# Six places where TensorE waits in a graph-attention and attention kernel: a store reordered behind a read, and work moved or turned at the two ends

## The chip, the cores and the metric

The kernel runs on one core of a Trainium2 chip. The metric is the device time in microseconds of one execution; three executions of the kernel before took 3074.83, 3075.51 and 3082.33 us. A core has five engines that work side by side, each in the order of its own instruction list: TensorE (PE) for matrix products, VectorE (DVE), ScalarE (ACT), GpSimd (POOL), and SyncE (SP), which here only issues DMAs. They wait for one another through semaphores.

## The reference

x holds 32 batches of 512 nodes with 512 features; adj is one 512 x 512 mask for all. Two layers follow each other, each with a residual and a layer norm without weights:

```python
# layer 0: one graph attention head of width 256
h = x @ W                                            # 512 -> 256
e = leaky_relu((h @ a[0]) + (h @ a[1]).T, 0.2)       # 512 x 512
out = softmax(e + NEG * (1 - adj)) @ h
x = layernorm(x + concat([out, h]))
# layer 1: eight heads of width 64
q, k, v = split(x @ Wq.T + bq), split(x @ Wk.T + bk), split(x @ Wv.T + bv)
attn = softmax(where(adj == 0, -inf, q @ k.T / 8))
x = layernorm(x + merge(attn @ v) @ Wo.T + bo)
```

All is float32. The 32 batches don't depend on each other.

## The kernel before, in words

A batch b is worked in four passes of a pair of heads, hp = 0 to 3; (b,hp) names one pass. A pass makes the scores of both heads for four blocks of 128 queries (`head_scores`, L684): a matmul (L699), the row minimum of the masked negative scores on VectorE (L315), the exponential with its sum on ScalarE (L708). The weights so made must be turned, keys to partitions, before they can multiply the values. There are two ways:

- `head_blocks` (L720): VectorE transposes blocks of 32 x 32 (L330), eight instructions a pair, and SP issues 16 DMAs of 128 KB (L347) that move the blocks from tile t to their places in tile pt. There is one buffer of t and one of pt.
- `head_turn` (L729): TensorE transposes the eight tiles as matmuls with the identity (32 of them, L736) into PSUM, and VectorE and ScalarE copy four tiles each into pt (L737). The set `turned` (L981) lists the pairs done so.

The product of one pair with the values, `head_values` (L751, the matmuls of tile pav at L757), stands in the pass after it, behind that pass's scores. It is multiplied on VectorE (L769) by the inverse sums, which go through memory: written by SP as d_tot (L717), read back by GpSimd's queue (L748).

Between these stand the other parts, cut in steps and laid out by hand: the projections of queries and keys (`project_two`, tile pw, L545, four products per half batch with copies L569 by ScalarE and an add L598 by GpSimd) and of values (`project_v`, pv); layer 0 of the batch after (`l0_...`, tiles ph, et, po); and the end of the batch before: seven products of the output weights (`finish_seven`, pf, L789), the statistics (L280), `out_norm` (L890; two small steps on VectorE, then four activations L900) and `store` (L908). Every engine runs its instructions in the order in which the program lists them, and SP its DMAs likewise, so a DMA that has to wait holds back those behind it. A DMA also waits until the eighth one before it on SP's queue has landed. Buffers come from pools that turn round: x has three, so `load_x(b + 2)` writes where batch b - 1 lay, and waits for its store.

Layer 0 of batch b + 2 is begun in the pass hp = 3 of batch b: `l0_columns` writes the two attention columns to memory and reads them back as rows on all partitions (L389, L391); `l0_maxima` finds each row's bound; `l0_write` (L421, 2 KB) and `l0_read` (L426, 256 KB) bring it back as a row, from which `l0_row` (L434, GpSimd) makes a term of the scores in the next batch's first pass. `l0_weights` (L466) subtracts it and takes exponentials, `l0_values` (L472) makes the product po. `l0_add_h` (L375) adds h to the residual, four GpSimd instructions.

The opening (L922 to L964) does batch 0's layer 0, batch 1's projection in four products (`second`), and `x1_first` (L501), which turns the normed x of batch 0 with TensorE, four tiles px, each copied by ScalarE (L510). The end (L1095 to L1106) makes the last batch's output product directly: `last_products` (L853) adds the residual and three of four blocks of features, `last_product` the fourth, which needs the last pair, and `last_norm` norms each block and stores it.

Of the kernel before, what the change touches and what calls it, by code (L numbers as in the profile page):

```python
# [26 lines left out]
def kernel(  # L27
# [117 lines left out]
    def load_x(b):  # L145
        x_sb = io.tile([P, NB, F], F32, name=f"x_{b}", tag="x", bufs=3)
        nc.sync.dma_start(x_sb, x[b].rearrange("(c p) f -> p c f", p=P))
        st["x1", b] = x_sb
# [17 lines left out]
    for g in range(4):  # L166
        nc.sync.dma_start(
            adjp_sb[g * G : (g + 1) * G],
            adj[g * P : (g + 1) * P].rearrange("(i q) n -> q i n", q=G),
        )  # L170
    nc.sync.dma_start(wo_sb, wot.rearrange("(c p) d -> p c d", p=P))
    load_x(1)
    nc.gpsimd.dma_start(bq_sb, bq)
    nc.gpsimd.dma_start(bk_sb, bk)
    with nc.allow_non_contiguous_dma(reason="512 numbers, once"):
# [182 lines left out]
    def l0_product(b, i):  # L358
        xt_sb = st["xt", b]
        ph = ps_m.tile([P, 2 + F1], F32, name=f"ph_{b}_{i}", tag="m")  # L360
        matmul_f(ph, lambda c: xt_sb[:, c, i * P : (i + 1) * P], lambda c: w_sb[:, c, :])
        return ph
# [12 lines left out]
    def l0_add_h(b):  # L375

        h_sb, z = st["h", b], st["x1", b]
        for i in range(NB):
            nc.gpsimd.tensor_tensor(
                z[:, i, F1:], z[:, i, F1:], h_sb[:, i, 2 : F1 + 2], ALU.add  # L380
            )
# [42 lines left out]
    def l0_read(b):  # L424

        nc.sync.dma_start(  # L426
            st["rows", b][:, 1], st["least", b].partition_broadcast(P)
        )
# [69 lines left out]
        move_one(x1t.rearrange("p g c (i q) -> p g c i q", i=NB), t)  # L498
        st["x1t", b] = x1t

    def x1_first():  # L501

        z = st["x1", 0]
        x1t = act.tile([P, 4, FC, NB * G], F32, name="x1t_0", tag="x1t")
        for i in range(NB):
            px = psum_s(f"px_{i}")
            for c in range(FC):
                cols = slice(c * P, (c + 1) * P)
                nc.tensor.transpose(px[:, cols], z[:, i, cols], ident)
            nc.scalar.copy(  # L510
                x1t[:, :, :, i * G : (i + 1) * G].rearrange("p g c q -> p c g q"),
                px.rearrange("p (c g q) -> p c g q", c=FC, g=4),
            )
        st["x1t", 0] = x1t
# [236 lines left out]
    def head_values(b, hp, bank=None):  # L751
        pt, inv = st.pop(("pt", b, hp)), st.pop(("inv", b, hp))
        po = (bank or psum)(f"pav_{b}_{hp}")
        for c in range(NB):
            for j in range(2):
                head = 2 * hp + j
                nc.tensor.matmul(  # L757
                    po[j * D : (j + 1) * D, :],
                    st["v", b, c // 2][:, c % 2, head * D : (head + 1) * D],
                    pt[:, :, j, c, :, :].rearrange("p g i q -> p g (i q)"),  # L760
                    start=(c == 0),
                    stop=(c == NB - 1),
                )
        if hp % 2 == 0:
            st["ot", b, hp // 2] = act.tile(
                [P, 2, N], F32, name=f"ot_{b}_{hp // 2}", tag="ot", bufs=3
            )
        ot = st["ot", b, hp // 2][:, hp % 2]
        nc.vector.tensor_tensor(  # L769
            ot.rearrange("p (g i q) -> p g i q", g=4, i=NB),  # L770
            po.rearrange("p (g i q) -> p g i q", g=4, i=NB),
            inv.rearrange("p (g q) i -> p g i q", g=4),
            ALU.mult,
        )
# [133 lines left out]
    def store(b):  # L908
        nc.sync.dma_start(out[b].rearrange("(c p) f -> p c f", p=P), st["x1", b])
# [7 lines left out]
    def steps(todo):  # L917
        for _ in todo:
            pass
# [18 lines left out]
    for i in range(NB):  # L938
        l0_values(0, i)
        ln_stats(st["x1", 0], "0_0", i)  # L940
        if i == NB - 1:
            second.append(l0_product(1, 3))
            for k in range(NB):
                l0_copy(1, k, second[k])
        ln_root("0_0", [i])
        if i == 1:
            weight_negative(QUERIES)
        if i > 0:
            l0_norm(0, [i - 1])
    l0_norm(0, [NB - 1])  # L950
    x1_first()
    l0_columns(1)
    x1_sums(0, nc.vector)
    weight_sums(VALUES, nc.vector)
# [23 lines left out]
        nc.vector.tensor_tensor(bo_sb, pb, bo_sb, ALU.add)  # L978

    before = None  # L980
    turned = {(B - 2, 2), (B - 1, 2), (B - 1, 3)}  # L981
    for b in range(B):
        more = b < B - 1
        seven = finish_seven(b - 1) if b > 0 else None
        for hp in range(NP):

            head_scores(b, hp, 0)
            head_scores(b, hp, 1)  # L990
            if hp == 0:
                values = project_v(b)
                next(values)
                if more:
                    l0_scores(b + 1, [0, 1])
                if b == 0:
                    l0_add_h(1)
            elif hp == 1:
                if b == 0:
                    l0_output(1)  # L1000
                else:
                    if more:
                        l0_weights(b + 1)
                    next(seven)
            elif hp == 2:
                if b > 0:
                    next(seven)
                if b > 0 and more:
                    add_bias(b + 1)
            else:  # L1010
                if b > 0:
                    if b + 2 >= B:
                        steps(seven)
                    if not more:
                        output_weights()
                    out_stats(b - 1)
                else:
                    weight_sums(OUTPUT, nc.gpsimd)
                    add_bias(0)
                if b + 2 < B:  # L1020
                    for i in range(NB):
                        l0_project(b + 2, i)
                    l0_columns(b + 2)
                if b > 0:
                    ln_root(f"1_{b - 1}")
            head_scores(b, hp, 2)
            head_scores(b, hp, 3)
            if b > 0 and hp in (1, 2):
                next(seven)
            if b > 0 and hp == 3:  # L1030
                out_norm(b - 1)
            if (b, hp) not in turned:
                head_blocks(b, hp)
            if before is not None:
                head_values(*before)
            if (b, hp) in turned:
                head_turn(b, hp)
            if hp == 0:
                if more:
                    l0_row(b + 1)  # L1040
                    leaky(st["row", b + 1])
                next(values)
                head_inverse(b, 0)
                if b > 0 and more:
                    l0_add_h(b + 1)
                if more:
                    l0_scores(b + 1, [2, 3])
                steps(values)
                if b == 0:
                    l0_weights(1)  # L1050
            elif hp == 1:
                head_inverse(b, 1)
                if b > 0 and more:
                    next(seven)
                    l0_output(b + 1)
                if b + 2 < B:
                    load_xt(b + 2)
                two = project_two(b, 1)
                next(two)
                if more:  # L1060
                    l0_norm(b + 1)
                next(two)
                blocks = x1_blocks(b + 1) if more else None
                for part in (blocks, two, blocks, two, blocks):
                    if part:
                        next(part, None)
                if not more:
                    next(seven)
            elif hp == 2:
                if b == 0:  # L1070
                    output_bias()
                else:
                    next(seven)
                    if b + 2 < B:
                        steps(seven)
                head_inverse(b, 2)
                if more:
                    x1_sums(b + 1, nc.gpsimd)
            else:
                if b + 2 < B:  # L1080
                    l0_maxima(b + 2)
                    l0_write(b + 2)
                if b > 0:
                    store(b - 1)
                if b + 2 < B:
                    l0_read(b + 2)
                    load_x(b + 2)
                if more:
                    steps(project_two(b + 1, 0))
                head_inverse(b, 3)  # L1090
                if b == 0:
                    weight_negative(OUTPUT)
                    add_bias(1)
            before = (b, hp)
    b = B - 1  # L1095
    for i in range(NB):
        last_products(b, i)
    head_values(b, 3, psum_s)
    norms = []
# [66 lines left out]
```

## Time and profile before

| | |
|---|---|
| median of three executions | 3075.51 us |
| the profiled execution's own time | 3080.21 us |
| its span, first to last instruction | 3078.4 us |
| TensorE busy | 3039.4 us |
| VectorE, ScalarE, GpSimd busy | 2490.8, 1537.7, 1251.6 us |
| mean granted clock of TensorE | 0.996 |
| DMA issues of pt moves | 2000, 128 KB each, landing after 3.4 us (median) |

A profile is one execution. Busy time is the time in which an engine executed; what it waited for stands in the list of waits, as `engine tile line <- releaser: us in total, times, longest us`. A line of the timeline reads: start, duration, engine, line of the kernel, operation, `out<-in` tiles, shape, the count of merged instructions, and in brackets the idle time before the first and what ended it. A duration of merged instructions runs from the first start to the last end, or to the window's edge. DMAs stand as issues of the queue SPq. The granted clock says which share of TensorE's full rate it was given in a stretch.

### The profile page before, as it was taken

Reading aid. Unit: us, or ns where it says so; the run is one execution under the profiler, and the core shown is the slowest. Engines: PE = TensorE matmul, PEld = TensorE weight load, DVE = VectorE, ACT = ScalarE, POOL = GpSimd, SP = SyncE. Lnnn points to the kernel's source line nnn. Section 1 sums busy time; section 2 is a strip of 40 time slices with the busy share of each in tenths; the row PEclk is TensorE's granted clock in tenths of the full one; section 3 lists DMA queues with packets and bytes.
Section 4 is the critical chain, followed back from the end, with each engine's and each line's share of the span. In section 5 each row is a group of like instructions: output and inputs, shape, how many; then the busy total and the mean of one; then the engine's idle time right before and its main releaser. Section 6 shows DMA issues by size and latency. Waiting matters only on the chain. (4 is left out here: it accounts for less than half of the span.)

```text
span 3078.4 us, 44731 instructions
## 1 busy us (share of the span) xinstructions
PE 3039.4 (99%) x13460; PEld 2065.7 (67%) x13460; DVE 2490.8 (81%) x5711; ACT 1537.7 (50%) x3262; POOL 1251.6 (41%) x1224
## 2 busy tenths in 40 slices
PE   8999999999999999999999999999999999999998
PEld 6566666666666666666666666666666666666654
DVE  6788888888878887888888888878888888888865
ACT  4355554545544545544455545455444555454544
POOL 4343444443343434444433434344444334343422
PEclk9999999999999999999999999999999999999999
DMA  6556666566575666665666755666656667556632
GB/s 180 142 138 157 156 164 154 138 164 159 145 177 135 152 156 160 159 158 136 168 155 147 176 142 148 156 156 158 160 138 168 151 150 177 143 143 155 157 93 66
DMA packets 245633, 464.64 MB, mean 151 GB/s; under 512 B 94800, under 2 KB 97360, under 8 KB 245392
## 3 DMA queue, kind: packets, MB, share of 16 engines
q1 hardware_dynamic: 232928, 427.93, 56.1%
q0 software_dynamic: 12464, 33.84, 4.1%
q8 instruction: 109, 1.79, 0.3%
q14 instruction: 132, 1.08, 0.1%
HBM read 132.65 MB, written 34.27 MB: 54 GB/s over the span
## 5 line engine op out<-in xcount | busy, mean ns | idle before, releaser
L708 ACT ACTIVATE p<-p,least 128x512 f32<-128x512 f32 x1024 | 725.8, 711 | 509.8 <-DVE least L315 192.7
L315 DVE CUSTOM_DVE_ANT_0 p<-ps,mask 128x512 f32<-128x512 f32 x1024 | 644.9, 685 | 219.0 <-PE ps L699 218.7
L330 DVE STREAM_TRANSPOSE t<-p 128x512 f32<-128x512 f32 x1000 | 607.7, 674 | 10.2 <-issue 5.5
L699 PE MATMUL ps<-qk 64*128 64x512 f32 x2048 | 511.3, 615 | 0.3 <-DVE least L315 0.3
L757 PE MATMUL pav<-pt,v 128*64 128x512 f32 x2048 | 469.8, 600 | 12.7 <-DMA d_att<-att 6.2
L748 POOL DMA_DIRECT2D inv<-d_tot x256 | 134.4, 530 | 587.3 <-DMA d_tot<-tot 273.7
L757 PEld LDWEIGHTS pav<-pt,v 128*64 128x64 f32 x2048 | 139.2, 137 | 328.8 <-issue 289.6
L699 PEld LDWEIGHTS ps<-qk 64*128 64x128 f32 x2048 | 179.3, 186 | 206.3 <-issue 152.2
L459 POOL TENSOR_TENSOR et<-et,mask0t 128x512 f32<-128x512 f32 x126 | 143.9, 1155 | 324.7 <-ACT et L455 324.7
L812 POOL TENSOR_TENSOR x<-x,u_o 128x512 f32<-128x512 f32 x93 | 117.0, 1273 | 303.2 <-ACT u_o L807 271.8
L477 PE MATMUL po<-h,et 128*128 128x257 f32 x1024 | 234.0, 387 | 3.5 <-ACT et L470 2.9
L264 PE MATMUL ph<-w_sb,xt 128*128 128x258 f32 x1024 | 235.0, 387 | 0.3 <-DVE w_sb L190 0.3
L477 PEld LDWEIGHTS po<-h,et 128*128 128x128 f32 x1024 | 190.3, 191 | 59.8 <-issue 28.0
L264 PEld LDWEIGHTS ph<-w_sb,xt 128*128 128x128 f32 x1024 | 193.3, 191 | 51.4 <-PE ps L699 22.0
L534 POOL TENSOR_TENSOR x<-x,bo_sb 128x512 f32<-128x512 f32 x128 | 158.5, 1271 | 92.0 <-DVE x1t_b L330 92.0
L708 ACT ACTIVATION_READ_ACCUMULATOR p<-p,least 128x1 f32 x1024 | 192.5, 188 | 0.0
L708 ACT ACT_TABLE_LOAD x63 | 80.8, 1283 | 220.0 <-DVE least L315 219.5
L286 ACT ACTIVATE rstd<-mv,eps 128x4 f32<-128x4 f32 (+1 forms) x66 | 19.6, 297 | 335.8 <-DVE mv L281 332.8
L789 PE MATMUL pf<-wo_sb,ot 128*128 128x256 f32 x744 | 182.2, 388 | 0.0
L789 PE MATMUL pf<-wox_sb,ot 128*128 128x256 f32 x744 | 179.0, 383 | 0.0
L789 PEld LDWEIGHTS pf<-wo_sb,ot 128*128 128x128 f32 x744 | 136.2, 190 | 63.0 <-DVE least L315 23.5
L280 DVE BATCH_NORM_STATS2 stats<-x 128x6 f32<-128x512 f32 x252 | 171.8, 682 | 7.8 <-POOL x L812 3.0
(155 smaller groups left out, 5386.1 us busy)
## 6 DMA issues: line engine op xcount, KB each, us to landing
pt<-t SPq DMA_DIRECT2D x2000, 128.0 KB, 3.4
x<-in_x_dram SPq DMA_DIRECT2D x32, 1024.0 KB, 5.6
inv<-d_tot POOLq DMA_DIRECT2D x256, 128.0 KB, 3.8
xt<-in_xt_dram SPq DMA_DIRECT2D x31, 1024.0 KB, 5.4
x1t<-x1t_b SPq DMA_DIRECT2D x496, 64.0 KB, 2.0
out_dram<-x SPq DMA_DIRECT2D x31, 1024.0 KB, 5.7
rows<-d_att SPq DMA_DIRECT2D x31, 512.0 KB, 3.8
rows<-d_least SPq DMA_DIRECT2D x31, 256.0 KB, 4.2
```

Source lines behind the costliest of these rows:

```text
L264: nc.tensor.matmul(ps, lhs(c), rhs(c), start=(c == 0), stop=(c == FC - 1))
L280: nc.vector.bn_stats(stats, z[:, i, :])
L315: nc.vector.tensor_tensor_reduce(out=out, in0=scores, in1=mask, scale=-1.0, scalar=MIN_INIT, op0=ALU.add, op1=ALU.min, accum_out=least,)
L330: nc.vector.transpose(t[:, :, :, i, :].rearrange("p r c q -> p c r q"), src.rearrange("p (c r k) -> p c r k", r=4, k=G),)
L459: engine.tensor_tensor(et[:, j, :], et[:, j, :], mask0t[:, j, :], ALU.add)
L477: nc.tensor.matmul(po, et[:, j, i * P : (i + 1) * P], h_sb[:, j, 2:], start=(j == 0), stop=(j == NB - 1),)
L534: nc.gpsimd.tensor_tensor(z[:, i, :], z[:, i, :], bo_sb, ALU.add)
L699: nc.tensor.matmul(ps, qk[rows, 0, i * P : (i + 1) * P], qk[rows, 1, :], start=True, stop=True)
L708: nc.scalar.activation(p, p, AF.Exp, bias=least, scale=-1.0, accum_out=total[:, j, i : i + 1])
L748: nc.gpsimd.dma_start(inv[j * D : (j + 1) * D], d[j].partition_broadcast(D))
L757: nc.tensor.matmul(po[j * D : (j + 1) * D, :], st["v", b, c // 2][:, c % 2, head * D : (head + 1) * D], pt[:, :, j, c, :, :].rearrange("p ...
L789: nc.tensor.matmul(ps[:, k * half : (k + 1) * half], columns[:, c, k * P : (k + 1) * P], weights(c), start=start and k == 0 and c == 0, st ...
```

## The change

Six edits:

- **Opening, loads.** x of batch 1 is loaded ahead of the output weights wo_sb.
- **Opening, layer 0.** The fourth product of batch 1's projection moves from ahead of all four px tiles to between the second tile's transposes and its copy. Its copy to h and `l0_add_h(1)` follow `x1_first`; the latter stood in pass (0,0), behind the first scores of batch 1's layer 0.
- **Pair (0,2)** is turned by TensorE: `head_turn` in place of `head_blocks`, and so behind `head_values(0,1)` rather than ahead of it.
- **Each batch's end, on SP:** `l0_write`, `l0_read`, `store`, `load_x`, where `store` stood ahead of `l0_read`. This concerns batches 1 to 29.
- **Batch 30:** `out_norm(29)` moves from behind the scores of pass (30,3) into `project_two(31, 0)`, behind its first step with its four copies on ScalarE; `store(29)` follows it.
- **Batch 31:** `out_norm(30)` and `store(30)` move behind the loop. The first two `last_products` move ahead of the turning of pair (31,3).

```diff
+    load_x(1)
     nc.sync.dma_start(wo_sb, wot.rearrange("(c p) d -> p c d", p=P))
-    load_x(1)
...
-    def x1_first():
+    def x1_first(between):
...
                 nc.tensor.transpose(px[:, cols], z[:, i, cols], ident)
+            if i == 1:
+                between()
             nc.scalar.copy(
...
         if i == NB - 1:
-            second.append(l0_product(1, 3))
-            for k in range(NB):
+            for k in range(NB - 1):
                 l0_copy(1, k, second[k])
...
-    x1_first()
+    x1_first(lambda: second.append(l0_product(1, 3)))
+    l0_copy(1, 3, second[3])
+    l0_add_h(1)
     l0_columns(1)
...
-    turned = {(B - 2, 2), (B - 1, 2), (B - 1, 3)}
+    turned = {(0, 2), (B - 2, 2), (B - 1, 2), (B - 1, 3)}
...
-                if b == 0:
-                    l0_add_h(1)
...
-            if b > 0 and hp == 3:
+            if b > 0 and hp == 3 and b + 2 < B:
                 out_norm(b - 1)
             if (b, hp) not in turned:
                 head_blocks(b, hp)
             if before is not None:
                 head_values(*before)
+            if (b, hp) == (B - 1, 3):
+                last_products(b, 0)
+                last_products(b, 1)
             if (b, hp) in turned:
                 head_turn(b, hp)
...
                 if b + 2 < B:
                     l0_maxima(b + 2)
                     l0_write(b + 2)
-                if b > 0:
+                    l0_read(b + 2)
+                if b > 0 and b + 2 < B:
                     store(b - 1)
                 if b + 2 < B:
-                    l0_read(b + 2)
                     load_x(b + 2)
                 if more:
-                    steps(project_two(b + 1, 0))
+                    two = project_two(b + 1, 0)
+                    next(two)
+                    if b + 2 >= B:
+                        out_norm(b - 1)
+                        store(b - 1)
+                    steps(two)
...
     b = B - 1
-    for i in range(NB):
+    out_norm(b - 1)
+    store(b - 1)
+    for i in (2, 3):
         last_products(b, i)
```

## The prediction

> **What bounds the kernel now.** First the page: busy shares, then the 40 slices.
>
> ```profile
> PE 3039.4 (99%) x13460; PEld 2065.7 (67%) x13460; DVE 2490.8 (81%) x5711; ACT 1537.7 (50%) x3262; POOL 1251.6 (41%) x1224
> PE   8999999999999999999999999999999999999998
> ```
>
> TensorE sets the time; only the first and last slices show it idle. So the second view is the list of its own waits, longest in total first (total us, times, longest).
>
> ```profile
> PE pav L757 <- DMA d_att<-att: 6.2, 2, 5.0
> PE pw L545 <- ACT p L569: 4.8, 1, 4.8
> PE pav L757 <- DMA d_least<-least: 3.6, 4, 1.5
> PE po L477 <- ACT et L470: 2.9, 1, 2.9
> PE px L509 <- DVE rstd L291: 1.6, 1, 1.6
> PE pt L736 <- DVE pt L737: 1.5, 2, 1.2
> ```
>
> These are nearly all the 39 us that TensorE is not busy (3078.4 - 3039.4), and each can be looked up in the timeline. The edits sit at these six places. The pav that waited "for d_att" waits for the pair (0,2), whose last move lands 0.3 us before it.
>
> ```profile
> 67.58 2.60 POOL L379 TENSOR_TENSOR x<-x,h 128x256 f32<-128x256 f32 x4
> 70.14 2.11 POOL L434 TENSOR_TENSOR row<-rows 128x512 f32<-128x512 f32 x1
> 77.44 2.38 ACT L470 ACTIVATE et<-et 128x512 f32<-128x512 f32 x4 [4.54 <-DVE et L469]
> 78.21 9.21 PE L477 MATMUL po<-h,et 128*128 128x257 f32 x32 [2.86 <-ACT et L470]
> ...
> 133.55 5.77 PE L757 MATMUL pav<-pt,v 128*64 128x512 f32 x16 [4.99 <-DMA d_att<-att]
> ...
> 2959.35 2.91 ACT L900 ACTIVATE x<-x,shift,rstd 128x512 f32<-128x512 f32 x4
> 2962.17 1.53 ACT L569 COPY p<-pw 128x512 f32<-128x512 f32 x3
> 2962.88 2.05 PE L545 MATMUL pw<-tx,wqx_sb 128*128 128x256 f32 x4 [4.75 <-ACT p L569]
> ...
> 3024.83 3.90 PE L736 MATMUL pt<-ident,p 128*128 128x128 f32 x32
> ```
>
> A second cost hides behind the long waits: the work after them is slow (pav 5.77 us instead of 3.65, four pw matmuls 2.05 instead of 1.03). The granted clock by 5 us window was 0.73 and 0.93 from 40 us, 0.68 from 80, 0.60 and 0.72 from 130, 0.57 and 0.75 from 2960, and 1.00 nearly everywhere between.
>
> The last place recurs. SP's queue at the end of one batch:
>
> ```profile
> 2030.51 0.53 SPq L421 DMA_DIRECT2D d_least<-least  x1
> 2031.15 0.38 SPq L909 DMA_DIRECT2D out_dram<-x  x1
> 2035.13 0.33 SPq L426 DMA_DIRECT2D rows<-d_least  x1
> 2037.20 0.37 SPq L147 DMA_DIRECT2D x<-in_x_dram  x1
> 2040.10 0.36 SPq L717 DMA_DIRECT2D d_tot<-tot  x1
> ```
>
> The store goes out 1.3 us after the last move of pair (b,3); the move landed 4.4 us after the write's issue, the pav at 2034.94 waited 1.47.
>
> **The skill.** The Trainium skill, "TensorE: Matmul & The Clock Gate", Part 1 (The HAM clock gate), says the array falls to half rate after a mostly idle window of about 3.4 us, and stays there until a busy one. The trace agrees: each low stretch above sums to about 3.4 or 6.8 us at half rate ((1-0.60)x5 + (1-0.72)x5 = 3.4 us of clock lost). "DMA: Bandwidth & Descriptors", Queues, rings and completion order, says that a DMA's semaphore lands only after every earlier write of the same DMA engine. The trace agrees: the 2 KB write landed in 1.40 us in the opening, but in 3.3 to 4.6 us in most batches, behind moves and beside the store. "SBUF — State Buffer", Who interferes with whom, says a GpSimd operation and a VectorE one in a two-port mode exclude each other; here the norm L296 took 1.07 us at 36.82 beside GpSimd work and 0.55 elsewhere.
>
> **The change, part by part** (us on TensorE's own order).
>
> *Opening, px.* The fourth product of batch 1 (8 matmuls, 1.91) moves into the 1.56 hole behind px1. px2 still waits for VectorE's norms (40.14), and pw for the last copy (42.18), so nothing is gained directly. But TensorE is then busy some 2.5 of the 3.4 us before 42.3 instead of 1.3, so the half-rate window (42.3 to 45.7, 1.7 lost) should go. Against it: the four adds of h (2.60) now run on GpSimd from 39.1, beside the norms at 39.59 and 40.24, which I charge 0.8 (twice the 0.5 seen at 36.82, part of it in slack). x of batch 1 is issued ahead of wo_sb to be there; wo_sb is not read until about 114. The fourth copy and att come about 0.5 later on ScalarE, hidden by GpSimd's busy p add before L404. Net -0.9 (0 to -1.7).
>
> *h added early.* The row L434 starts at 67.6 instead of 70.14. Then VectorE's leaky starts at 70.05 instead of 72.29; value results to 74.15; subtractions 74.15 to 76.9, the last two paced by GpSimd's masks, which end at 76.0 (its inverse issue still waits for d_tot, 72.6). Exponentials end at 77.6 instead of 79.8: -2.2. The half-rate window from 79.8 (1.7) should go too. But VectorE then is the limit: statistics end 85.6 instead of 89.0, 3.4 earlier, and pair (0,1), with 0.54 of slack at its pav, follows VectorE. -3.5 (-2 to -4).
>
> *Pair (0,2) turned.* Added on TensorE: 32 transposes, 3.90 as at 3024.83. Removed: the wait 4.99 and half rate in the pav, 5.77 - 3.65 = 2.12. VectorE gives 8 block transposes (4.86) for 4 copies (about 2.7), ScalarE takes 4 copies (2.4) in a gap of 6.2, SP loses 16 moves (10 us). 3.90 - 7.11 = -3.2. The pav then comes at 132.4, and pw at 136.0 finds tx ready (GpSimd, 129.8). Next late would be pair (0,3): slack 5.06, of which 3.2 and 0.6 (its blocks start later) are used. Range -2 to -4.
>
> *Read, then store, then load.* 29 times. Removed: the store from beside the last moves of (b,3). From their last issue those land in 3.49 on average, the other pairs' in 2.93 to 3.14. The (b,3) waits sum to 4.5 over nine batches; I expect 3.2 of it to go. Added: SP now waits for the write's landing (about 2.5) before the store, so the load, which waits for the store (about 5.7), goes out some 2.3 later, at 8.6 after the write instead of 6.3. Behind it on SP stand d_tot and the 16 moves of (b+1,0), released by VectorE at 8.9 to 10.8: just free. The load lands 3.7 after the first move instead of 1.4; the seventh move needs its landing and goes at 3.7. Over 30 batches the landing of the last move hardly follows the load's (correlation 0.34), so I take 0.4 later; the slack of (b,0) is 1.7 on average, 0.45 at least: 0.2 lost in all. -3.0 (+23 to -4.5; see the rivals).
>
> *Norms behind the copies, batch 30.* The four L900 (2.91) go behind p1, p5, p7, u2. p1 ends at 2959.95, TensorE resumes at 2960.05 instead of 2962.88, and part or all of the slow 2.3 goes. But pair (30,3) lands at 2975.6, 0.35 earlier now that VectorE skips two small steps, against a pav at 2977.99: no more than 2.4 + 0.35. -2.7 (-1.5 to -4).
>
> *End.* From the end of pav (31,2), 3043.26, to pav (31,3), 3063.69, are 20.4. The work in it is 3.9 of transposes and 4 x 3.44 = 13.8 of products. Two products (6.9) now cover the exponentials (done at 3046.7) and the copies; their third block needs ot (31,2) at 3045.8, ready at 3045.4. -2.8. The inverses should land near 3061.5, 3 before they are used; the norms and store of batch 30 run under the last products.
>
> Sum: -0.9 - 3.5 - 3.2 - 3.0 - 2.7 - 2.8 = -16.1, in the profiled execution 3078.4 to 3062.3 of span. Its own time was 3080.2, 4.7 above the median 3075.5 of the three runs, which all I expect to shift alike: 3059.4.
>
> **Rivals.** *The load comes too late (slower).* At the head of each (b,0) the load and the moves share the DMA engines. If the last move follows the load fully, 2.3 late, the 29 slacks in the trace leave 18.3 of waits, and I land at 3075.5 - 13.1 + 18.3 = 3080.7; at 2.5 late 23.7 and 3086. It decides from 2.0 late on (11.2 of waits, no gain left to measure). For it: the seventh move waits for the load. Against: moves go one per 0.63 us, so a backlog drains, and load landings from -0.1 to +2.8 left the last move at 12.3 to 13.9. *The opening's gains are absorbed.* VectorE is over 90% busy from 90 to 120; if half rate stays in the opening and (0,2) finds GpSimd or SP behind it, 7.6 there become 2, and the end 3065. *The tail and batch 30 are held by landings:* pair (30,3) or the inverses come late, 4 lost: 3063.4. *Reorder without effect* (other traffic makes the tails late): 3062.4.
>
> **How the numbers follow.** Forecast, everything roughly as summed, 0.66; no effect of the reorder or landings in the tail 0.14; opening absorbed 0.10; load too late 0.10, half of it slower. About 0.3%, 9.2 us, is what a measurement can tell from no change, so faster means under 3066.3. It follows from the first two cases and 0.05 of the third: 0.85; slower 0.05; the same 0.10. The range: part ranges added in quadrature give about 4; downward all half-rate windows gone, 3053; upward the absorbed opening and a load 1.5 late (3.3 of waits), 3069.
>
> **What would show it.** Right: no wait above 1 us at po near 76, at pav (0,2), at pt of the last pair; no half-rate stretch near 80 and 131; 1984 moves instead of 2000 and 992 block transposes instead of 1000; L900 of batch 30 behind L569; the read issued 2.5 after the write. Wrong: new waits of pav (b,0) behind x<-in_x_dram, or a pair (0,3), (30,3) that takes over the wait.

## The result and the profile after

The changed kernel is slower: 3086.90 us median of 8 executions (3082.68 to 3089.06) against 3076.39 (3074.08 to 3082.33) for the kernel before on the same chip, a ratio of 1.0030 [1.0019, 1.0041]. Forecast were 3059.4 us and a range of 3053 to 3069. The profiled execution took 3083.0 us (3080.21 before), one of the shortest of the eight; its span is 3081.2 us (3078.4).

The page first, its busy shares and the row of TensorE in 40 slices.

```profile
PE 3038.7 (99%) x13492; PEld 2070.5 (67%) x13492; DVE 2530.2 (82%) x5707; ACT 1549.4 (50%) x3266; POOL 1249.4 (41%) x1224
PE   8999999999999999999999999999999999999999
```

TensorE does 0.7 us less and the last slice is now full, so the end did improve. The span is 2.8 longer all the same. TensorE's waits, in the form in which they were shown of before (total us, times, longest):

```profile
PE pav L759 <- ACT et L470: 10.0, 12, 2.6
...
PE pav L759 <- DMA pt<-t: 3.5, 7, 0.9
PE pav L759 <- issue: 3.2, 4, 2.0
PE po L477 <- ACT et L470: 2.2, 1, 2.2
...
PE pw L547 <- ACT p L571: 1.9, 1, 1.9
PE px L509 <- DVE inv L485: 1.5, 1, 1.5
```

Of the two long ones, the one that was put down to d_att (5.0 us at the pair (0,2)) is gone, and the one behind p is 1.9 instead of 4.8. In their place stand many small waits of pav, most of them put down to the exponentials of the next batch's layer 0 (L470). That is not what they wait for: seven of these products begin before the last of those exponentials has ended. But each one that waited begins 0.1 to 0.5 us after the landing of its pair's sixteenth move. Sorted by pair, the idle time before pav is, in us over the whole run: pairs (b,0) 0.0 before, 14.5 after; (b,2) 8.2 and 2.8; (b,3) 4.5 and 2.8.

The places of the forecast, from the timeline (start, duration, engine, line, operation, tiles, shape, and the idle time before):

```profile
65.92 2.16 POOL L434 TENSOR_TENSOR row<-rows 128x512 f32<-128x512 f32 x1
75.17 2.38 ACT L470 ACTIVATE et<-et 128x512 f32<-128x512 f32 x4 [3.93 <-DVE et L469]
75.95 7.56 PE L477 MATMUL po<-h,et 128*128 128x257 f32 x32 [2.24 <-ACT et L470]
...
128.26 3.65 PE L759 MATMUL pav<-pt,v 128*64 128x512 f32 x16
...
2967.24 1.13 PE L547 MATMUL pw<-tx,wqx_sb 128*128 128x256 f32 x4 [1.90 <-ACT p L571]
2970.39 2.93 ACT L902 ACTIVATE x<-x,shift,rstd 128x512 f32<-128x512 f32 x4 [0.53 <-DVE shift L898]
2982.18 5.35 PE L759 MATMUL pav<-pt,v 128*64 128x512 f32 x16 [2.00 <-issue]
...
3056.04 3.66 PE L738 MATMUL pt<-ident,p 128*128 128x128 f32 x32
3071.30 3.70 PE L863 MATMUL pf<-wo_sb,ot 128*128 128x512 f32 x8 [1.15 <-DVE ot L771]
```

The product po starts 2.26 earlier and runs in 7.56 us instead of 9.21, at full clock. The pav of (0,2) waits for nothing, at full clock. In batch 30 the norms stand behind the copies, but the pair (30,3), which the forecast named as the limit there, is now late by 2.00 us.

So the opening works in this execution. The pav of (1,0) starts at 171.52 instead of 178.92, 7.4 earlier. From there the lead melts: 6.3 us at (2,0), 2.8 at (10,0), and a lag of 5.4 at (20,0) and of 7.2 at (30,0). That is 14.6 us lost over 29 batches, half a microsecond each on average. From (30,0) to the last instruction the changed kernel gains 4.4 (171.9 us against 176.3). The loss recurs (23 of the 29 products of (2,0) to (30,0) wait, up to 2.6 us), and SP's queue at the same batch end as shown of before says where:

```profile
2035.52 0.52 SPq L421 DMA_DIRECT2D d_least<-least  x1
2038.79 0.34 SPq L426 DMA_DIRECT2D rows<-d_least  x1
2039.22 0.39 SPq L911 DMA_DIRECT2D out_dram<-x  x1
2044.96 0.38 SPq L147 DMA_DIRECT2D x<-in_x_dram  x1
2045.47 0.42 SPq L719 DMA_DIRECT2D d_tot<-tot  x1
2046.06 11.08 SPq L347 DMA_DIRECT2D pt<-t  x16
```

The store leaves 3.7 us behind the write instead of 0.6, and the load 9.4 instead of 6.7, so that it is only 1.1 ahead of the first move (before: 3.4). Two lines of SP's waits show what is behind it; the first existed before as 67.8 us in 29 waits, the second did not exist.

```profile
SPq L147 <- DMA out_dram<-x: 162.5, 29, 7.5
SPq L347 <- DMA x<-in_x_dram: 23.7, 25, 1.9
```

In the first line the load waits for the landing of the store, 5.6 us a batch instead of 2.3. Then a move waits for the landing of the load. It is the seventh one, eight DMAs behind the load. In all 29 batches it goes out at the load's landing or within 0.6 us of it, in 26 of them 0.01 to 0.02 us after. The product at the end of this chain, of the pair whose moves start at 2040.63 before and at 2046.06 after, had no wait before (first line) and has one after:

```profile
2056.57 3.65 PE L757 MATMUL pav<-pt,v 128*64 128x512 f32 x16
2061.08 3.65 PE L759 MATMUL pav<-pt,v 128*64 128x512 f32 x16 [0.60 <-DMA pt<-t]
```

### The profile page after: what moved, and what is told of

It is laid out like the page before. It is cut to its first block, busy times and chain, and to the rows that moved or that the text cites. A ratio compares the mean times of both kernels' runs of the same rounds, so it can differ in the third digit from the quotient of the medians.

```text
span 3081.2 us, 44770 instructions
## 1 busy us (share of the span) xinstructions
PE 3038.7 (99%) x13492; PEld 2070.5 (67%) x13492; DVE 2530.2 (82%) x5707; ACT 1549.4 (50%) x3266; POOL 1249.4 (41%) x1224
## 4 chain that ended last, share of the span: by engine, by line
PE 83%; DVE 7%; DMA 3%; SPq 3%; issue 2%; ACT 1%; POOL 1%; DVEq 0%; ACTq 0%; POOLq 0%
PE pw L547 23%; PE pav L759 13%; PE ps L701 12%; PE pv L623 11%; PE pf L791 10%; PE ph L264 7%; PE po L477 6%; SPq L347 2%; DVE t L330 2%; DVE p L315 2%; DVE et L469 1%; DMA pt<-t 1%; ACT et L470 1%; DMA x<-in_x_dram 1%; DMA out_dram<-x 1%
## 5 line engine op out<-in xcount | busy, mean ns | idle before, releaser
L315 DVE CUSTOM_DVE_ANT_0 p<-ps,mask 128x512 f32<-128x512 f32 x1024 | 644.5, 684 | 206.7 <-PE ps L701 206.5
L536 POOL TENSOR_TENSOR x<-x,bo_sb 128x512 f32<-128x512 f32 x128 | 158.4, 1269 | 90.3 <-DVE x1t_b L330 90.2
```

The lines of the kernel that those rows point to most:

```text
L315: nc.vector.tensor_tensor_reduce(out=out, in0=scores, in1=mask, scale=-1.0, scalar=MIN_INIT, op0=ALU.add, op1=ALU.min, accum_out=least,)
L536: nc.gpsimd.tensor_tensor(z[:, i, :], z[:, i, :], bo_sb, ALU.add)
```

## The experiments

Theory 1: the new order makes the load late, the late load makes the moves of pair (b+1,0) late, and TensorE waits for them. Its rivals: the loss comes from the store's traffic, from the tail, or from the opening. All ratios are to the kernel before on the same chip.

**The old order back.** The changed kernel with SP's old order.

```diff
                     l0_write(b + 2)
-                    l0_read(b + 2)
                 if b > 0 and b + 2 < B:
                     store(b - 1)
                 if b + 2 < B:
+                    l0_read(b + 2)
                     load_x(b + 2)
```

> The changed kernel with SP's old order, store ahead of the read; all other edits stay. Theory (the load that goes out late delays the moves of each pair (b,0), and this alone made the kernel slower): the waits of pav at (b,0) go, the opening's 7.4 and the end's 4.4 us are kept, so about 11 us faster than before, near 3065. Rival (the other edits brought TensorE forward into landings that then stop it, whatever SP's order): the gain of the opening melts over the batches again, 0 to 4 us faster than before at most.

Measured: 3073.51 us (3067.59 to 3081.12, 13 executions), 0.9989 [0.9981, 0.9997]. The waits before pav in (b,0) are 0.0 again, and the lead over before is 6.5 at (1,0) and 7.1 at (30,0): it no longer melts. So the order is what costs. But the median is well above its own profiled execution of 3067.59.

**The new order alone** in the kernel before.

```diff
                     l0_write(b + 2)
+                if b + 2 < B:
+                    l0_read(b + 2)
                 if b > 0:
                     store(b - 1)
                 if b + 2 < B:
-                    l0_read(b + 2)
                     load_x(b + 2)
```

> The kernel before with the read ahead of the store, and nothing else. Theory (late load): about 14 us slower than before over 29 batches, near 3090, with waits of pav at (b,0) and waits of the moves for the load of x. Rival (the other edits brought TensorE forward into landings): within 3 us of before, or up to 4 us faster since the waits at (b,3) go.

Measured: 3099.39 us, 1.0069 [1.0056, 1.0083], some 22 us dearer. Idle time before pav in (b,0): 17.6 us; in (b,3), where the forecast saw its gain, 0.7 instead of 4.5. The gain of 3.8 is there, and the new waits are nearly five times as large.

**The load late, the store early.** To part the load's lateness from the store's: before's order, with three 2 KB transfers in a chain (SBUF to memory, back, and out again) between read and load. The result computed is the same.

```diff
+    def delay(b):
...
+        nc.sync.dma_start(d, st["sb_least", b])
+        nc.sync.dma_start(s, d)
+        nc.sync.dma_start(e, s)
...
                     l0_read(b + 2)
+                    if b > 0:
+                        delay(b + 2)
                     load_x(b + 2)
```

> The kernel before, with the store in its old place, ahead of the read, and three tiny DMAs of 2 KB, each waiting for the one before, between the read and the load of x: the load goes out some 2 to 3 us later, the store and the read do not. Theory (it is the load's lateness): slower than before by 12 us or more, with the same waits at (b,0), as the waits at (b,3) stay too. Rival (it is the store, whose traffic now falls between the load and the moves, or the earlier read): within 3 us of before.

Measured: 3200.74 us, 1.0397 [1.0383, 1.0411]. TensorE's waits for pav in (b,0) are 87.1 us; the half-rate stretches become many, and the clock makes up the rest of the 123: its mean of 0.985 over 3200.5 us means some 48 us lost, against 12 before (0.996 over 3078.4). So a late load costs without any change to the store's place. How much of this is the load's landing alone is not shown: the chain also holds SP's queue, so that the first move goes out 1.4 us later than before (table below), and its small transfers run beside the load.

**The load less late.** The same with the first small transfer ahead of the read; `delay` now yields behind it.

```diff
                     l0_write(b + 2)
                 if b > 0:
                     store(b - 1)
                 if b + 2 < B:
+                    late = delay(b + 2) if b > 0 else None
+                    if late:
+                        next(late)
                     l0_read(b + 2)
+                    if late:
+                        steps(late)
                     load_x(b + 2)
```

> The kernel before, with the store in its old place and the load put off by the same three small transfers as in the run that put it off by 4.4 us, but with the first of them ahead of the read, so that the load goes out about 1.3 to 1.8 us later than before: between 7.6 and 8.1 us behind the write of the maxima, where the new order has 9.25. The result computed is the same. The load's lateness as the only cause, with a slack of about 1.7 us at the last move and a loss only beyond some 2 us of lateness: 0 to 6 us slower than before (3078 to 3084). A loss in proportion to the lateness (20 us at 2.9): 9 to 12 us. A loss of 15 us or more would say that the small transfers themselves are what costs.

Measured: 3146.64 us, 1.0217 [1.0195, 1.0239], some 66 us dearer. The load's lateness missed its aim: the load went out 9.43 us behind the write, not 7.6 to 8.1, because each hop of the chain took longer than I had reckoned. So the run says nothing of where a loss begins. By the expectation's last sentence a loss this large speaks for a cost of the small transfers themselves, and that is not ruled out: the load was sent at nearly the same time as in the new order, but took 7.3 us to land instead of 6.1, and the waits before pav in (b,0) are 52.3 us, three times those of the new order alone. What made it land later, the small transfers or something else, was not measured apart.

**The load on another queue.** Is it the seventh move's wait, or the load's traffic beside the moves? The changed kernel (with the bias of batch 1 moved, see below) with the load issued by GpSimd, so that no move stands behind it.

```diff
-                if b + 2 < B:
-                    load_x(b + 2)
...
                 head_inverse(b, 3)
+                if b + 2 < B:
+                    load_x(b + 2, nc.gpsimd)
```

> The changed kernel with the output bias of batch 1 moved (3086.6 us) and, besides, the load of x(b+2) issued by GpSimd behind the broadcast of the last pass's sums, and no longer by SyncE; store and read keep their new order, and the load still waits for the store's landing. Theory A (the moves of pass (b+1, 0) come late because the seventh of them stands in SyncE's queue until the load has landed: 5.04 us behind the first, against 3.97 in the old order): the seventh move is back at about 4.0 us behind the first, the waits before the product of pass (b, 0) fall from 18.9 us to under 5, and the time by 14 to 20 us, to 3066 to 3073. Theory B (the load's 1 MB, now 3.3 us later, takes the moves' share of the transfer engines, whichever queue issues it): the last move stays 1.5 us or more late, and the time at 3082 to 3088. A third outcome: GpSimd, held until the store has landed, is late with the mask of the next attention (line 459), and the attention's products wait: over 3090.

Measured: 3157.06 us, 1.0259 [1.0245, 1.0273]. The seventh move is indeed back at 4.12 us behind the first, but from there to the sixteenth it then takes 8.4 us instead of 6.1 (same kernel with the load on SP), the load 8.3 instead of 6.3, and the last move lands at 26.57 instead of 24.97. Theory A's gain did not come: without the wait on the load nothing is better. But the run does not show that this wait is harmless in the changed kernel, since the edit slowed the load and the moves as well. The first six moves took 6.2 to 7.8 us to land, on average, instead of 5.1 to 5.7, and the ninth to eleventh, which need the landings of the first three, went out within 0.1 us of these in 11 to 18 of the 29 batches (0 to 2 with the load on SP): one wait took the place of another. It is not clean for theory B either, since GpSimd itself is held (its wait for the store in the first line, then TensorE's for the moves):

```profile
POOL x L147 <- DMA out_dram<-x: 399.1, 25, 17.4
PE pav L759 <- DMA pt<-t: 41.9, 18, 3.9
```

The six runs together give one table. Means over 29 batches, in us behind the issue of the write of the maxima; the last two columns are the time by which the last move of (b+1,0) lands later than before, and TensorE's idle time before that pav, per batch.

| kernel | load out | load lands | 7th move behind 1st | last move lands | later | waited |
|---|---|---|---|---|---|---|
| before | 6.33 | 11.95 | 3.89 | 23.24 | | 0.00 |
| after | 9.25 | 15.40 | 4.90 | 24.98 | 1.74 | 0.50 |
| new order alone | 9.35 | 15.44 | 4.79 | 24.94 | 1.70 | 0.61 |
| load less late | 9.43 | 16.71 | 6.14 | 26.48 | 3.24 | 1.80 |
| load late | 10.69 | 18.04 | 6.34 | 27.63 | 4.39 | 3.00 |
| load on GpSimd | 9.28 | 17.60 | 4.12 | 26.57 | 3.33 | 2.29 |

Lateness less wait is 1.0 to 1.4 us in all five: on average a slack of that size, and what goes beyond it is paid in full, 29 times. Where the load is on SP and lands late, its landing is also the place of the seventh move: first move plus the fourth column is 15.45, 16.73 and 18.06 for after and the two late loads (first moves at 10.55, 10.59 and 11.72), against landings of 15.40, 16.71 and 18.04.

**The opening alone**, in the kernel before: the loads' order, the fourth product, the early h and the pair (0,2).

```diff
-    turned = {(B - 2, 2), (B - 1, 2), (B - 1, 3)}
+    turned = {(0, 2), (B - 2, 2), (B - 1, 2), (B - 1, 3)}
...
+    l0_add_h(1)
...
```

> The kernel before with the edits of the opening and of pair (0,2) alone. Theory: 7 us faster than before, near 3069: TensorE's lead of 7.4 us at pav (1,0) is carried to the end. Rival (an earlier TensorE meets landings): the lead melts, 0 to 3 us.

Measured: 3078.70 us, 0.9999 [0.9991, 1.0007]. The 7.4 us are not there at all, and its pav of (1,0) starts at 179.36. In that trace one of VectorE's four bounds of batch 2 (L315 of `l0_maxima`, from pass (0,3)) takes 6.03 us instead of 0.69, while GpSimd does the four adds of the output bias of batch 1 (`add_bias(1)`, L536). This gave theory 2: the opening's edits bring the bound and these adds together, and the lead is lost in that collision. A further profile of the changed kernel shows the same:

> The changed kernel again, for one more profile. If the collision of the bound with the bias costs it as it costs the old order with the new opening, one of the four bound instructions of batch 2 (line 315, near 137 us) takes 5 to 6 us and the first product with the values of batch 1 begins at 177 us or later. If it is free of it in most executions (moving the bias gave it 0.3 us), it begins near 171.5 again, and the 29 batches after it lose 17 to 21 us.

```profile
140.15 6.02 DVE L315 CUSTOM_DVE_ANT_0 junk<-pn,mask 128x512 f32<-128x512 f32 x1
140.69 4.93 POOL L536 TENSOR_TENSOR x<-x,bo_sb 128x512 f32<-128x512 f32 x4
143.24 1.03 PE L547 MATMUL pw<-x1t,wkx_sb 128*128 128x256 f32 x4
147.81 3.39 PE L701 MATMUL ps<-qk 64*128 64x512 f32 x8 [3.54 <-DVE qk L584]
```

In the kernel before, bound and adds were clear of one another:

```profile
142.80 0.69 DVE L315 CUSTOM_DVE_ANT_0 junk<-pn,mask 128x512 f32<-128x512 f32 x1
147.68 4.94 POOL L534 TENSOR_TENSOR x<-x,bo_sb 128x512 f32<-128x512 f32 x4
```

In the changed kernel the bound stands in front of VectorE's adds that make qk, so TensorE's next scores wait 3.54 us and then run at half clock (3.39 instead of 1.99). The execution took 3094.87 us, and its pav of (1,0) starts at 176.60, 5.1 later than in the first profile. The Trainium skill, "SBUF — State Buffer", Who interferes with whom, says that a VectorE instruction with two inputs in SBUF contends with a GpSimd instruction that reads SBUF. These bounds have pn and the mask in SBUF. The bounds of the scores, with one input in PSUM, take 0.69 us everywhere. In the first profile of the changed kernel the last bound ended at 140.20 and the adds began at 140.66, so half a microsecond decided. In the kernel before, 4.2 us lie between them (143.49 and 147.68): there GpSimd, ahead of the adds, waited 4.47 us for a copy of ScalarE (its add L598).

A further execution of the old order in the changed kernel agreed:

> The changed kernel with SyncE's old order again, for one more profile. The theory of the collision (moving the bias gave it 6.4 us): one of the four bound instructions of batch 2 takes 5 to 6 us, the first product with the values of batch 1 begins at 177 us or later, and the time is 3072 to 3077. Rival: no long bound instruction, a begin near 172.5, and a time of 3072 to 3077 all the same, so that the 6 us come from elsewhere.

It has a bound of 6.02 us, the pav of (1,0) at 177.92, and took 3072.13 us, near the median of its earlier executions.

**The bias moved.** The adds go one batch later, behind the columns of batch 3, in four kernels.

```diff
                     l0_columns(b + 2)
+                if b == 1:
+                    add_bias(1)
...
                     weight_negative(OUTPUT)
-                    add_bias(1)
```

> The kernel before with the opening's edits and the pair (0, 2) turned by TensorE, as in the run of the opening alone, and the output bias of batch 1 moved. Theory: the opening's 7.4 us, which were nowhere in that run (0.9999 [0.9991, 1.0007]), come out: 3069 to 3071 us against 3076 to 3077 before, a ratio of 0.998. The first product with the values of batch 1 (a row of the output product, line 701 or 759) begins about 7 us before the 178.92 us of before. Rival: 3075 to 3079, no gain.

> The kernel before with only the output bias of batch 1 moved in the same way. In the profile of before the bound's four instructions (140.96 to 143.4 us) end 4.3 us before the adds begin (147.68), so the theory expects no change: within 1.5 us of the kernel before. Rival (the adds in that place are dear in themselves, or their new place is cheaper or dearer for some other reason): a gain of 3 us or more here too, or a loss.

> The changed kernel with SyncE's old order, and the output bias of batch 1 (four adds of 128x512 on GpSimd, 4.94 us) moved from the end of batch 0's last pass to batch 1's last pass, behind the columns of batch 3. Theory (the bound of batch 2's rows on VectorE, line 315, now begins 2 to 5 us earlier and falls together with these adds[...], so that in most executions one of its four instructions stands for some 6 us and the opening's gain of 7.4 us is gone again): 5 to 7 us below the same kernel with the adds in their old place, so 3066 to 3068 us by the median against 3073.5, near its own profiled execution of 3067.6, and with less spread over its runs than the 13.5 us there; each of the four bound instructions 0.7 us. Rival (the loss lies elsewhere, or was chance in one execution): 3072 to 3075, with the same spread.

> The changed kernel itself with only the output bias of batch 1 moved. Theory: the collision goes, the late load stays: 3080 to 3083 us, against 3086.9 for the changed kernel, so still 4 to 7 us slower than before. Rival: 3085 to 3088.

| on one chip | us | ratio to before (3077.81) |
|---|---|---|
| before, bias moved | 3078.14 | 0.9996 [0.9988, 1.0004] |
| opening alone, bias moved | 3072.62 | 0.9982 [0.9975, 0.9988] |
| after in the old order, bias moved | 3067.07 | 0.9960 [0.9946, 0.9973] |
| after, bias moved | 3086.59 | 1.0026 [1.0018, 1.0034] |

The first three are as theory 2 says. The opening alone gains 6.1 by the move (3078.70 to 3072.62), the old order 6.4 (3073.51 to 3067.07), the kernel before nothing. The fourth is a miss: the changed kernel itself gained 0.3 by the medians (3086.90 to 3086.59, on two chips), or 1.7 when each is taken against the kernel before on its own chip (10.5 and 8.8 us above it), where 4 to 7 was expected. The third beats the kernel before by 10.7 us, and the changed one by more. A further single execution of it gave 3064.73.

> A second look at the old order with the output bias of batch 1 moved (3067.07 us by the median), beside the run of the load on GpSimd: 3064 to 3070; nothing is changed in it, and it serves as the row to compare with.

**The miss, side by side** on one chip.

> The changed kernel, timed beside itself with the output bias of batch 1 moved. If the collision costs it as it does the old order: 3090 to 3094 us, and 5 to 7 us above the other. If the late load absorbs what the collision would cost (a batch that is behind elsewhere waits less for its load): both within 2 us, and the two profiles differ mainly in what the batches lose after the first.

> The changed kernel with the output bias of batch 1 moved: 3085 to 3088 us, whichever of the two holds; its profile has four short bound instructions, a begin of the first product with the values of batch 1 near 171 us, and waits before the products of pass (b, 0) of 17 to 21 us.

Measured: after 3096.51 us (3086.97 to 3098.26), 1.0048 [1.0035, 1.0061]; with the bias moved 3093.26 (3089.87 to 3095.70), 1.0040 [1.0026, 1.0054]. The ranges overlap, and 3.2 us lies between the two expectations. The profile of after has the bound of 6.02 us and its pav of (1,0) 5.3 later than that with the bias moved (177.25 against 171.94), but loses 21.5 us in the 29 batches against 25.7. The granted clock accounts for as much: with the bias moved those batches hold three stretches of 3.4 us at half rate, 1.7 lost in each; with the bias in its old place they hold none. Whether that is chance, one profile of each cannot tell. With the bias in its old place, two of the three profiles of the changed kernel show the bound of 6.02 us, and so does one of the two of the old order. What the collision costs the changed kernel by the median, 1.7 us in one comparison and 3.2 in the other, and why it is less than the 6.4 of the old order, stays open. On this chip the kernel with the bias moved was 12.8 us above before, against 8.8 on the other; why is not known.

## Why the prediction was wrong

The sign was wrong, and one step did it; a second step made the miss larger. From the runs on one chip the whole falls into three parts: the opening 3077.81 to 3072.62, -5.2; batch 30 and the end 3072.62 to 3067.07, -5.5; the new order 3067.07 to 3086.59, +19.5. Their sum is +8.8, against +10.5 measured for the change on another chip. These runs have the bias moved. With the bias in its place, as in the change itself, the old order is 3.8 below before and the new one 10.5 above it, so that the order cost 14.3, and all the other edits together gained 3.8 instead of the 13.1 forecast.

- **Read, then store, then load: forecast -3.0, measured +19.5** (14.3 with the bias in its place, 22 for the new order alone). This is the step that failed. Its gain was right: the idle time at (b,3) goes from 6.1 to 1.3 us between the old and the new order with the bias moved (forecast 3.2). Its chain was right up to the last link: SP waits for the write, the store goes later, the load waits for it, and the seventh move needs its landing. The sizes were a little short: the load goes out at 9.25 us behind the write (forecast 8.6) and lands 4.9 behind the first move (3.7). The failing link is "the landing of the last move hardly follows the load's (correlation 0.34), so I take 0.4 later". It landed 1.74 later. The correlation came from the profile of the old order, where the load lands 1.6 us behind the first move on average and 2.8 at most. The seventh move leaves at 3.89 on average, at least 1.0 us behind that landing in each of the 29 batches, so the landing was past when its turn came. The correlation was taken where the wait does not bind, and used where it does. Of the 1.74, the seventh move's place behind the first is 1.0, the first move's own lateness 0.2, and the landing of the last, which took longer, 0.5. Nothing was caught up: from the seventh move to the sixteenth it is 6.1 us in both orders. Whether the moves would have been late by as much from the load's traffic alone, without the seventh move's wait, stays open; the load on GpSimd says that this can happen.
- **The rival "the load comes too late"** named the place and the wait, and got 0.10. That its 3080.7 to 3086 lies so near the 3086.9 measured is in part luck. It let the last move be 2.3 to 2.5 us late, with 18.3 to 23.7 of waits (11.2 at 2.0); measured are 1.74 late and 14.5 of waits. And it kept 13.1 of gains elsewhere, of which 3.8 came. The argument against it, that a backlog drains at 0.63 us a move, fails because that is the pace of issue, and the moves kept to it: nine steps in 6.1 us, some 0.68 each, in both orders.
- **Opening: forecast -7.6.** The trace of the changed kernel gives -7.4 at (1,0): -3.9 at (0,0) against -4.4 for px and h together, and -3.5 against -3.2 for the pair (0,2). That the first of these fits is in part luck of the half-rate stretches. Those near 42, 80 and 131 are gone in this trace, as expected; but of the twelve profiles with the opening's edits seven keep one of 3.4 us at 76 to 77. And the new order alone, whose opening is that of before, has none near 42, and its pav of (0,0) at 86.69 instead of 89.27. With the bias moved in both, the pav of (0,0) goes from 88.52 to 87.02 and that of (1,0) from 178.65 to 173.13, which is -5.5. By the medians it is -5.2, and only with the bias moved; without, there is no gain (0.9999, with the interval across 1). The step was incomplete: the two-port rule was quoted and priced beside the norms at 39 us, but not followed to 140 us, where the edits bring the bounds of batch 2 (4.4 earlier) up against the bias of batch 1 (7.0 earlier). The rival "absorbed" had a loss of 5.6, but by another cause.
- **Batch 30 and the end: forecast -2.7 and -2.8, together -5.5.** Measured -5.5 by the medians. In the trace the wait at pw falls by 2.85 and one of 2.00 at (30,3) comes in, with a half-rate stretch of 3.4 us where there were 6.8 behind pw; from pav (30,0) to the last instruction 4.4 are gained.
- **Two readings** do not hold as written, though no sum rests on them. The six waits that the prediction lists are not nearly all of the 39 us in which TensorE is not busy. They sum to 20.6; 5.0 lie ahead of its first product and 6.2 behind its last. And the Trainium skill, "TensorE: Matmul & The Clock Gate", Part 1 (The HAM clock gate), which it quotes, speaks of an idle window; that a mostly idle one is enough is what this trace shows (TensorE was busy for some 1.3 of the 3.4 us ahead of the half-rate stretch at 42.3).
- **What the prediction told to look for** came out: no wait above 1 us at pav (0,2) or at pt of the last pair, 1984 moves, the read issued 2.7 us behind the write on average (forecast 2.5), and, under "wrong", new waits of pav (b,0). At po a wait of 2.24 us stayed, where none above 1 was promised.

## What to carry to other kernels

Moving a DMA back in an in-order queue is not priced by the DMA itself. Look for the first instruction behind it that needs its landing (here the seventh move), and for the transfers that then run at the same time. Before a correlation from the old profile is used, ask whether the constraint ever bound there; if not, work out where it begins to bind and take the full lateness beyond that. And when edits shift two engines by different amounts, look down the whole stretch for pairs of instructions that used to be clear of one another.

## What was not expected of the hardware

- A bound with both inputs in SBUF that had begun 0.54 us ahead of four GpSimd adds was recorded with 6.02 us, past the end of the last of them (140.15 to 146.17; the adds 140.69 to 145.62). It was 0.69 us without them, and 1.75 beside a single add of 1.6. It was held through all four, though it began first.
- With the load on GpSimd's queue, so that no move stands behind it, both the load and the moves were slower: the load took 8.3 us instead of 6.3, and the moves from the seventh to the sixteenth 8.4 instead of 6.1.
